# A fourth store tile, and weight splits of two pairs, in a kernel of 496 pairwise products

## The chip, the cores and the metric

The kernel runs on one core of a Trainium2 chip. The metric is the device time of one execution in microseconds (us). Five runs of the kernel before took 775.05 to 776.29 us, median 775.73.

## The reference

Each of 1024 samples has 32 fields of 128 numbers. For every pair of fields i < j (496 pairs) with a weight matrix of its own, field i goes through the matrix and the result is multiplied by field j, element by element:

```python
pairs = list(itertools.combinations(range(32), 2))
v_i = inputs[:, I_IDX, :]                    # (1024, 496, 128)
v_j = inputs[:, J_IDX, :]
transformed = jnp.einsum('bpd,ped->bpe', v_i, W)   # W: (496, 128, 128)
return transformed * v_j
```

The output, 1024 x 496 x 128 numbers of float32, is 260 MB. Everything else is small beside it: 32.5 MB of weights and 16.8 MB of input.

## The kernel before

**Layout.** The host hands over x transposed, one slab of 128 x 1024 for each field (d by sample), and the weights in the order in which the kernel uses them, four pairs to a transfer. All slabs of x stay in SBUF. The pairs are taken by rows: i runs down from 30 to 0, and for each i all j above it, so that the rows grow from 1 pair to 31. A pair is worked on in two halves of 512 samples; such a half is a unit u, and pair q has the units 2q and 2q + 1.

**Products.** The first 15 pairs (i from 30 to 26) are multiplied in float32 as they are (L148). All others use a faster number format in three matmuls: x and the weights are each split in a high part, a low part and a combination of both (h, l, d). In `first(u)` TensorE multiplies h by h and l by l into one PSUM bank (two matmuls, L151), and ScalarE scales the bank (L152). In `second(u)`, three units later (LAG = 3), TensorE adds the product of the d parts (L160), and VectorE multiplies the bank by x of field j into the store tile (L166). There are eight PSUM banks.

**Splits.** `split_w(c)` makes h, l and d for a chunk c of WC = 4 pairs: one ScalarE instruction for h (L92), then three of GpSimd (L93 for l, L94 and L95 for d), each 128 x 512. The three results are tiles of the pool `ws`, three tiles each. `split_x(f, a)` does the same for half a slab of x (L106 to L109), in the pool `xs`, two tiles each. All splits stand in the list `todo` with the pair from which they may be put out and the pair that needs them (L117 to L123). The list is sorted by need. After every odd unit at most one split is put out: the first in the list that may be. A split of chunk c may be put out from pair (c - 2) * WC + 1, that is 4c - 7, seven pairs ahead of pair 4c.

**Stores and loads.** A store tile `ot` holds two pairs (OG = 2), 128 x 2 x 1024, 1 MB. The pool `o` has three of them (L64). When VectorE has written the fourth product into it, SyncE issues its store (L170); the last two pairs are stored by halves (L168). SyncE also issues the loads of weights (L83, 256 KB for four pairs, in the pool `wr` of five tiles, four transfers ahead) and of x (L74, some rows ahead), all in one queue in order of program.

**Order.** From `tc.manual_schedule()` on, each engine executes its instructions in the order in which the loop over u writes them. What an engine waits for follows from the tiles: a store tile is written again when its last store has landed, a PSUM bank when VectorE has read it, a raw weight tile is loaded again when all its splits have read it.

**SBUF**, in KB of a partition: x 128, `xs` 24, `wr` 10, `ws` 18, `o` 24, together 204.

Of the kernel before, what the change touches and what calls it, by code (L numbers as in the profile page):

```python
# [1 line left out]

# [4 lines left out]

F32 = mybir.dt.float32
F32R = mybir.dt.float32r
ALU = mybir.AluOpType  # L10

P = 128
NF = 32
NQ = NF * (NF - 1) // 2
BT = 1024
HB = 512
WC = 4
WL = 4
OG = 2
EPS = 2.0**-12  # L20
NATIVE = 5
LAG = 3
WLEAD = 4
XLEAD = 3


def _pairs():

    return [(i, j) for i in range(NF - 2, -1, -1) for j in range(i + 1, NF)]


@with_exitstack
def kernel(
    ctx: ExitStack,
    tc: tile.TileContext,
    xt: bass.AP,
    wt: bass.AP,
    out: bass.AP,
):

    nc = tc.nc
    pairs = _pairs()
    nchunk = NQ // WC

    xpool = ctx.enter_context(tc.tile_pool(name="x", bufs=1))  # L60
    spool = ctx.enter_context(tc.tile_pool(name="xs", bufs=2))
    rpool = ctx.enter_context(tc.tile_pool(name="wr", bufs=5))
    wpool = ctx.enter_context(tc.tile_pool(name="ws", bufs=3))
    opool = ctx.enter_context(tc.tile_pool(name="o", bufs=3))  # L64
    ppool = ctx.enter_context(tc.tile_pool(name="ps", bufs=8, space=bass.MemoryType.PSUM))

    x_sb = {}

    def load_x(f, n=1, pieces=1, eng=None):

        t = xpool.tile([P, n, BT], F32, tag=f"x{f}", name=f"x_{f}")
        s = BT // pieces
        for k in range(pieces):
            (eng or nc.sync).dma_start(out=t[:, :, k * s : (k + 1) * s], in_=xt[:, f : f + n, k * s : (k + 1) * s])  # L74
        for k in range(n):
            x_sb[f + k] = t[:, k, :]

    w_raw = {}

    def load_w(c, splits=(0, WL)):  # L80
        w_raw[c] = rpool.tile([P, WL, P], F32, tag="w", name=f"w_{c}")
        for a, b in zip(splits, splits[1:]):
            nc.sync.dma_start(out=w_raw[c][:, a:b, :], in_=wt[c, :, a:b, :])  # L83

    w_s = {}

    def split_w(c):

        k = c * WC % WL
        raw = w_raw[c * WC // WL][:, k : k + WC, :].rearrange("p q e -> p (q e)")  # L90
        h, l, d = [wpool.tile([P, WC * P], F32R, tag=t, name=f"{t}_{c}") for t in ("wh", "wl", "wd")]
        nc.scalar.mul(h, raw, 1.0 - 2.0**-13)  # L92
        nc.gpsimd.tensor_tensor(l, raw, h.bitcast(F32), ALU.subtract)  # L93
        nc.gpsimd.tensor_scalar(d, h.bitcast(F32), EPS, 1.0, ALU.mult, ALU.mult)  # L94
        nc.gpsimd.tensor_tensor(d, l.bitcast(F32), d.bitcast(F32), ALU.subtract)  # L95
        w_s[c] = (h, l, d)

    x_s = {}

    def split_x(f, a):  # L100

        if a == 0:
            x_s[f] = [spool.tile([P, BT], F32R, tag=t, name=f"{t}_{f}") for t in ("xh", "xl", "xd")]
        s = slice(a, a + HB)
        h, l, d = [t[:, s] for t in x_s[f]]
        nc.scalar.mul(h, x_sb[f][:, s], 1.0 - 2.0**-13)  # L106
        nc.gpsimd.tensor_tensor(l, x_sb[f][:, s], h.bitcast(F32), ALU.subtract)  # L107
        nc.gpsimd.tensor_scalar(l, l.bitcast(F32), 1.0 / EPS, 1.0, ALU.mult, ALU.mult)  # L108
        nc.gpsimd.tensor_tensor(d, h.bitcast(F32), l.bitcast(F32), ALU.subtract)  # L109

    nq0 = NATIVE * (NATIVE + 1) // 2
    c0 = nq0 // WC
    first_q = {i: q for q, (i, j) in reversed(list(enumerate(pairs)))}

    todo = []  # L117
    for c in range(c0, nchunk):
        todo.append(((c - 2) * WC + 1, max(c * WC, nq0), lambda c=c: split_w(c)))
    for i in range(NF - 2 - NATIVE, -1, -1):  # L120
        for a in range(0, BT, HB):
            todo.append((first_q[i + 1] + 1 if i < NF - 3 - NATIVE else 2, first_q[i], lambda i=i, a=a: split_x(i, a)))
    todo.sort(key=lambda t: t[1])  # L123

    load_w(0, (0, 1, WL))
    load_x(NF - 2, pieces=2, eng=nc.scalar)
    load_x(NF - 1, pieces=2, eng=nc.scalar)
    load_x(NF - 3)
    load_x(NF - 4)
    load_w(1)  # L130
    for f in range(NF - 5, NF - 4 - XLEAD, -1):
        load_x(f)
    load_w(2)
    load_w(3)


    ctx.enter_context(tc.manual_schedule())
    po, ots = {}, {}


    def first(u):
        q, h = divmod(u, 2)
        i, c = pairs[q][0], q // WC
        r = slice(q % WC * P, (q % WC + 1) * P)
        s = slice(h * HB, (h + 1) * HB)
        po[u] = ppool.tile([P, HB], F32, tag="po", name=f"po_{u}")
        if q < nq0:
            nc.tensor.matmul(po[u], w_raw[q // WL][:, q % WL, :], x_sb[i][:, s], start=True, stop=True)  # L148
        else:
            for t in (0, 1):  # L150
                nc.tensor.matmul(po[u], w_s[c][t][:, r], x_s[i][t][:, s], start=t == 0, stop=t == 1)  # L151
            nc.scalar.mul(po[u], po[u], 1.0 + EPS)  # L152

    def second(u):
        q, h = divmod(u, 2)
        i, j = pairs[q]
        r = slice(q % WC * P, (q % WC + 1) * P)
        s = slice(h * HB, (h + 1) * HB)
        if q >= nq0:
            nc.tensor.matmul(  # L160
                po[u], w_s[q // WC][2][:, r], x_s[i][2][:, s], start=False, stop=True, skip_group_check=True
            )
        g, k = divmod(q, OG)
        if k == 0 and h == 0:
            ots[g] = opool.tile([P, OG, BT], F32, tag="ot", name=f"ot_{g}")
        nc.vector.tensor_tensor(ots[g][:, k, s], po.pop(u), x_sb[j][:, s], ALU.mult)  # L166
        if q >= NQ - 2:
            nc.sync.dma_start(out=out[g, :, k, s], in_=ots[g][:, k, s])  # L168
        elif k == OG - 1 and h == 1:
            nc.sync.dma_start(out=out[g], in_=ots[g])  # L170

    for u in range(2 * NQ + LAG):
        q = u // 2
        if u % (2 * WL) == 0 and (q // WL + WLEAD) * WL < NQ:
            load_w(q // WL + WLEAD)
        if u < 2 * NQ:
            i, j = pairs[q]
            if u % 2 == 0 and j == i + 1 and 0 <= i - 2 - XLEAD:
                load_x(i - 2 - XLEAD)
            first(u)  # L180
        if u >= LAG:
            second(u - LAG)
        if u % 2 == 1:
            ready = [t for t in todo if t[0] <= q]
            if ready:
                ready[0][2]()
                todo.remove(ready[0])
    assert not todo


# [25 lines left out]
```

## Time and profile before

| | before |
|---|---|
| median of five runs | 775.73 us |
| the profiled execution | 775.73 us |
| its span, first to last instruction | 773.9 us |
| moved by DMA | 310.04 MB, 260.05 written and 49.28 read in HBM |
| stores L170: count, size, issue to landing | 247, 1024 KB, 6.2 us |
| weight loads L83 | 123, 256 KB, 6.0 us |
| VectorE's product L166 | 992 of 684 ns |
| ScalarE's scaling L152 | 962 of 580 ns |
| ScalarE's split L92, 128 x 512 | 121 of 626 ns |
| GpSimd's split L93, L94, L95, 128 x 512 | 121 each, of 1289, 618 and 1295 ns |
| GpSimd's split of x, L107, L108, L109 | 52 each, of 1288, 619 and 1288 ns |

The profile is of one execution. A busy time counts the time in which an engine had an instruction running; instructions that follow each other closely overlap a little, so that four L166 of 684 ns take 2.48 us. PE is TensorE's matmuls, PEld its weight loads, DVE VectorE, ACT ScalarE, POOL GpSimd, SPq the queue of SyncE. In tables of waits each line says who waited (its line and tile), for whose result, and then the us in total, the number of waits and the longest. The DMA share of a stretch is the mean busy share of 16 DMA engines; it can be a little over 1, since packets overlap.

### The profile page before, as it was taken

The numbers are of one execution on the slowest core, as the hardware profiler recorded it, in microseconds if no ns is written. First come the engines' busy times: TensorE is split into PE (matmuls) and PEld (weight loads), VectorE is DVE, ScalarE is ACT, GpSimd is POOL, SyncE is SP. The second block draws the span as 40 slices with busy tenths as digits, with TensorE's granted clock in tenths as the row PEclk, the third lists the DMA queues.
The fourth block names the chain that finished last, engine by engine and source line by source line (L and its number), as shares of the span: only waits on it lengthen the run. The fifth ranks groups of instructions, "written<-read, shape, count | busy, mean of one in ns | idle before, by whom it ended". The sixth has DMA issues, their size and how long they took to land.

```text
span 773.9 us, 10983 instructions
## 1 busy us (share of the span) xinstructions
PE 719.1 (93%) x2946; PEld 549.8 (71%) x2946; DVE 617.6 (80%) x992; ACT 619.6 (80%) x1136; POOL 549.9 (71%) x523
## 2 busy tenths in 40 slices
PE   8979899998989999999998999898999999999996
PEld 3557676766767777677676877686877777777774
DVE  4668777777887787787787888787888888888886
ACT  2268788888968888888887888797998888888884
POOL 1978899887768767867767585767686859585550
PEclk9999999999999999999999999999999999999998
DMA  9999999999999999999999999999999999999998
GB/s 357 375 408 378 408 413 408 399 395 396 398 397 404 389 410 406 412 397 412 398 413 370 416 401 409 386 404 389 417 408 416 415 404 416 412 401 417 402 402 364
DMA packets 59101, 310.04 MB, mean 401 GB/s; under 512 B 6560, under 2 KB 6816, under 8 KB 27424
## 3 DMA queue, kind: packets, MB, share of 16 engines
q1 hardware_dynamic: 58464, 308.31, 99.2%
q10 hardware_dynamic: 576, 1.05, 0.4%
q8 instruction: 23, 0.38, 0.2%
q14 instruction: 38, 0.31, 0.1%
HBM read 49.28 MB, written 260.05 MB: 400 GB/s over the span
## 4 chain that ended last, share of the span: by engine, by line
DMA 47%; PE 30%; DVE 20%; issue 1%; DVEq 0%
DMA out_dram<-ot 47%; DVE ot L166 20%; PE po L151 20%; PE po L160 9%; PE po L148 1%; DMA x<-in_xt_dram 0%; DVEq L166 0%; DVEq L209 0%
## 5 line engine op out<-in xcount | busy, mean ns | idle before, releaser
L166 DVE TENSOR_TENSOR ot<-po,x 128x512 f32<-128x512 f32 x992 | 617.6, 684 | 150.4 <-DMA out_dram<-ot 105.4
L152 ACT ACTIVATE po<-po 128x512 f32<-128x512 f32 x962 | 540.6, 580 | 129.7 <-PE po L151 82.6
L151 PE MATMUL po<-xh,wh 128*128 128x512 f32 x962 | 390.3, 406 | 42.3 <-DVE ot L166 40.6
L151 PE MATMUL po<-xl,wl 128*128 128x512 f32 x962 | 379.1, 394 | 1.0 <-POOL wl L93 1.0
L160 PE MATMUL po<-xd,wd 128*128 128x512 f32 x962 | 378.6, 394 | 0.0
L151 PEld LDWEIGHTS po<-xh,wh 128*128 128x128 f32 x962 | 182.2, 189 | 122.6 <-DVE ot L166 84.0
L93 POOL TENSOR_TENSOR wl<-w,wh 128x512 fp32r<-128x512 f32 x121 | 156.0, 1289 | 154.0 <-ACT wh L92 154.0
L160 PEld LDWEIGHTS po<-xd,wd 128*128 128x128 f32 x962 | 182.4, 190 | 40.4 <-ACT po L152 0.4
L151 PEld LDWEIGHTS po<-xl,wl 128*128 128x128 f32 x962 | 182.7, 190 | 34.2 <-POOL wl L93 1.5
L95 POOL TENSOR_TENSOR wd<-wl,wd 128x512 fp32r<-128x512 f32 x121 | 156.7, 1295 | 10.1
L107 POOL TENSOR_TENSOR xl<-x,xh 128x512 fp32r<-128x512 f32 x52 | 67.0, 1288 | 22.8 <-ACT xh L106 22.8
L94 POOL TENSOR_SCALAR wd<-wh 128x512 fp32r<-128x512 f32 x121 | 74.8, 618 | 10.2
L92 ACT ACTIVATE wh<-w 128x512 fp32r<-128x512 f32 x121 | 75.8, 626 | 2.1 <-DMA w<-in_wt_dram 2.1
L109 POOL TENSOR_TENSOR xd<-xh,xl 128x512 fp32r<-128x512 f32 x52 | 67.0, 1288 | 4.3
L106 ACT ACTIVATE xh<-x 128x512 fp32r<-128x512 f32 x52 | 32.7, 630 | 11.7 <-DMA x<-in_xt_dram 11.6
L108 POOL TENSOR_SCALAR xl<-xl 128x512 fp32r<-128x512 f32 x52 | 32.2, 619 | 4.6
L148 PE MATMUL po<-x,w 128*128 128x512 f32 x60 | 28.0, 629 | 3.8 <-DMA x<-in_xt_dram 3.8
L148 PEld LDWEIGHTS po<-x,w 128*128 128x128 f32 x60 | 12.0, 202 | 18.9 <-issue 13.2
L106 ACT ACT_TABLE_LOAD x1 | 1.3, 1283 | 2.6 <-issue 2.6
L203 POOL MEMSET const-float32-0.0<- 128x1 f32 x1 | 0.1, 98 | 0.2 <-issue 0.2
L203 POOL MEMSET const-bfloat16-1.0<- 128x1 bf16 x1 | 0.1, 101 | 0.0
L203 POOL MEMSET const-uint8-127<- 128x1 uint8 x1 | 0.1, 101 | 0.0
(1 smaller groups left out, 0.1 us busy)
## 6 DMA issues: line engine op xcount, KB each, us to landing
out_dram<-ot SPq DMA_DIRECT2D x247, 1024.0 KB, 6.2
w<-in_wt_dram SPq DMA_DIRECT2D x123, 256.0 KB, 6.0
x<-in_xt_dram SPq DMA_DIRECT2D x30, 512.0 KB, 7.5
x<-in_xt_dram ACTq DMA_DIRECT2D x4, 256.0 KB, 4.7
out_dram<-ot SPq DMA_DIRECT2D x4, 256.0 KB, 4.6
w<-in_wt_dram SPq DMA_DIRECT2D x1, 192.0 KB, 3.5
w<-in_wt_dram SPq DMA_DIRECT2D x1, 64.0 KB, 2.7
```

The lines of the kernel that those rows point to most:

```text
L92: nc.scalar.mul(h, raw, 1.0 - 2.0**-13)
L93: nc.gpsimd.tensor_tensor(l, raw, h.bitcast(F32), ALU.subtract)
L94: nc.gpsimd.tensor_scalar(d, h.bitcast(F32), EPS, 1.0, ALU.mult, ALU.mult)
L95: nc.gpsimd.tensor_tensor(d, l.bitcast(F32), d.bitcast(F32), ALU.subtract)
L106: nc.scalar.mul(h, x_sb[f][:, s], 1.0 - 2.0**-13)
L107: nc.gpsimd.tensor_tensor(l, x_sb[f][:, s], h.bitcast(F32), ALU.subtract)
L109: nc.gpsimd.tensor_tensor(d, h.bitcast(F32), l.bitcast(F32), ALU.subtract)
L148: nc.tensor.matmul(po[u], w_raw[q // WL][:, q % WL, :], x_sb[i][:, s], start=True, stop=True)
L151: nc.tensor.matmul(po[u], w_s[c][t][:, r], x_s[i][t][:, s], start=t == 0, stop=t == 1)
L152: nc.scalar.mul(po[u], po[u], 1.0 + EPS)
L160: nc.tensor.matmul(po[u], w_s[q // WC][2][:, r], x_s[i][2][:, s], start=False, stop=True, skip_group_check=True)
L166: nc.vector.tensor_tensor(ots[g][:, k, s], po.pop(u), x_sb[j][:, s], ALU.mult)
```

## The change

- A chunk of split weights has two pairs instead of four (WC = 2). There are 241 splits in place of 121, each with the same four instructions, now 128 x 256.
- The pool `ws` has four tiles of each part in place of three: eight pairs of split weights in place of twelve, 12 KB a partition in place of 18.
- A split may be put out from pair (c - 3) * WC + 1, now 2c - 5, five pairs ahead of pair 2c.
- The pool `o` has four store tiles in place of three, 32 KB in place of 24. Together 206 KB in place of 204.

Loads (WL = 4 pairs to a transfer), stores, matmuls, L152 and L166 are the same in number and size.

```diff
-WC = 4
+WC = 2
...
-    wpool = ctx.enter_context(tc.tile_pool(name="ws", bufs=3))
-    opool = ctx.enter_context(tc.tile_pool(name="o", bufs=3))
+    wpool = ctx.enter_context(tc.tile_pool(name="ws", bufs=4))
+    opool = ctx.enter_context(tc.tile_pool(name="o", bufs=4))
...
-        todo.append(((c - 2) * WC + 1, max(c * WC, nq0), lambda c=c: split_w(c)))
+        todo.append(((c - 3) * WC + 1, max(c * WC, nq0), lambda c=c: split_w(c)))
```

## The prediction

> **What bounds the kernel now.** I read the page first, then the waits, then stretches of 2 us. Busy shares and the chain of waits:
>
> ```profile
> PE 719.1 (93%) x2946; PEld 549.8 (71%) x2946; DVE 617.6 (80%) x992; ACT 619.6 (80%) x1136; POOL 549.9 (71%) x523
> ...
> DMA packets 59101, 310.04 MB, mean 401 GB/s; under 512 B 6560, under 2 KB 6816, under 8 KB 27424
> ...
> DMA out_dram<-ot 47%; DVE ot L166 20%; PE po L151 20%; PE po L160 9%; PE po L148 1%; DMA x<-in_xt_dram 0%; DVEq L166 0%; DVEq L209 0%
> ```
>
> No compute engine sets the end alone: 47% of the chain is stores, and the DMA row of the page is 9 in nearly every slice. The table of waits says who feels it (us in total, times, longest):
>
> ```profile
> DVE ot L166 <- DMA out_dram<-ot: 105.4, 113, 4.2
> PEld po L151 <- DVE ot L166: 84.0, 117, 3.8
> ...
> PE po L151 <- DVE ot L166: 40.6, 35, 3.4
> ...
> PEld po L151 <- POOL wl L93: 1.5, 1, 1.5
> ...
> PE po L151 <- POOL wl L93: 1.0, 1, 1.0
> ```
>
> VectorE has no free store tile, TensorE no free PSUM bank behind it; GpSimd's splits cost TensorE only 2.5 us. But a wait for a transfer is worth something only if the DMA engines stand idle because of it later. The stretches of 2 us around the longest such wait show that (columns: busy us and instructions of PE, PEld, DVE, ACT, POOL, granted clock, DMA share, GB/s):
>
> ```profile
> 412.00:414.00 2.00, 2.00 (x11) 1.65 (x10) 2.00 (x4) 2.00 (x5) 1.90 (x3) 1.00 1.00 416
> 414.00:416.00 2.00, 1.92 (x9) 1.26 (x7) 0.33 (x1) 1.90 (x5) 1.93 (x2) 1.00 1.03 434
> 416.00:418.00 2.00, 0.00 (x0) 0.00 (x0) 0.00 (x0) 0.32 (x1) 1.83 (x3) 1.00 1.00 410
> 418.00:420.00 2.00, 0.72 (x3) 0.61 (x4) 1.46 (x3) 0.00 (x0) 1.92 (x3) 1.00 1.03 434
> 420.00:422.00 2.00, 2.00 (x8) 1.61 (x7) 2.00 (x4) 1.30 (x3) 1.85 (x2) 0.70 0.38 156
> 422.00:424.00 2.00, 2.00 (x6) 1.56 (x5) 1.47 (x3) 1.30 (x3) 0.00 (x0) 0.50 1.05 365
> ```
>
> While TensorE and VectorE stand still (414 to 419) the DMA runs at 410 to 434 GB/s: the wait itself costs nothing. The price comes after: the queue has emptied, TensorE starts again at half clock, and the DMA share falls to 0.38. So the bound is the DMA, and what can be had is the time in which it is not fed. I went through all stretches of 2 us from 28 to 768 us: 16 have a share under 0.90, and lack 7.2 us in all; 4 of the 7 under 0.80 have a lowered TensorE clock like this one. Another 54 have a share of 0.95 or more, yet under 390 GB/s; against the median stretch (414) they lose 16 us. Their cause no view names.
>
> **The fourth store tile (line 64).** A tile cycles through filling and storing. The median store lands 6.2 us after its issue, and four VectorE products take 2.48 us back to back, so three tiles give 8.7 us for six pairs, 1.45 us a pair against 1.56 (773.9 / 496) measured: the ring is only just long enough and any late store shows. A fourth adds 1 MB of queue, 2.5 us at 417 GB/s. It removes no byte: the best stretches of 20 us move 417 GB/s, and 310.04 MB at that rate is 743 us, a floor. I count the 7.2 us of missing share as what it can win, less the 2.3 us of it that lie before 160 us, where GpSimd gets in the way (below): **-5 us**. Of the 16 us of slow stretches the bounds are 0 (they come whatever the queue holds) and -16 (they come from a short queue). In the trace's packet records an 8 KB packet usually takes 309 ns, and in those stretches up to 606, twice that, as if a packet had no successor to overlap with; they sit mostly just ahead of a load that was issued behind a short queue. That speaks for the queue, only as a correlation: I take a third, **-5 us**.
>
> The Trainium skill speaks against any gain here: "DMA: Bandwidth & Descriptors", Specifications, gives a limit of about 358 GB/s of HBM for one core, by which nothing could be won, and a fabric ceiling of 435 GB/s, by which the floor would be 713 us. The trace's mean of 401 GB/s is above the first, so I don't count by it.
>
> **The finer splits (lines 17, 63, 119).** 121 splits of four pairs become 241 of two; each is one ScalarE and three GpSimd instructions, so 120 and 360 more instructions. No DMA is added. GpSimd's timeline at one piece of x and the split after it:
>
> ```profile
> 94.74 1.29 POOL L107 TENSOR_TENSOR xl<-x,xh 128x512 fp32r<-128x512 f32 x1
> 96.12 0.62 POOL L108 TENSOR_SCALAR xl<-xl 128x512 fp32r<-128x512 f32 x1
> 96.82 1.30 POOL L109 TENSOR_TENSOR xd<-xh,xl 128x512 fp32r<-128x512 f32 x1
> 98.07 1.30 POOL L93 TENSOR_TENSOR wl<-w,wh 128x512 fp32r<-128x512 f32 x1
> ```
>
> From 94.74 to 98.07 is 3.33 us for a split (2 x 1.29 + 0.62 + 0.13 of gaps). At 256 columns there is no row. Bounds: half of everything, 1.67 us, and no saving, 3.33 us. The nearest row for a fixed part is a MEMSET of one column, 98 to 101 ns: (1.29 - 0.10) / 2 + 0.10 = 0.70 and (0.62 - 0.10) / 2 + 0.10 = 0.36 us, so 2 x 0.70 + 0.36 + 0.13 = **1.88 us, 0.94 a pair** (0.83 before). GpSimd grows by 241 x 1.88 - 121 x 3.33 = 50 us, to some 600 of 774; the mean doesn't matter, the short rows at the start do. A row of n pairs costs it 6.67 us for two pieces of x and 0.94 n. The first L151 matmul of the rows of 6, 7, 8 ... pairs starts at 31.2, 42.0, 56.3, 69.1, 84.8, 99.5, 116.7, 136.1 and 156.3 us. Against these lengths (10.8, 14.3, 12.8, 15.7, 14.7 ...) GpSimd needs 12.3, 13.3, 14.2, 15.1, 16.1: its debt grows to 2.7 us at the row of 10, and is paid back by the row of 13. Before, 11.7, 12.5, 13.3, 14.2, 15.0 made a debt of 0.9 at most.
>
> The Trainium skill has a dearer price: "GPSIMD Engine Reference", 3.1, gives 4497 ns for a TENSOR_TENSOR of 2048 columns; with the 1289 ns of this trace at 512 that is an estimate of 754 ns at 256, a split of about 2.04 us, and a debt near 6 us instead of 2.7. No row here shows which holds.
>
> The lead shrinks with it. A split was put out 7 pairs ahead of its need (after unit 8c - 13, needed at 8c), now 5 (after 4c - 9, needed at 4c): 9 half-pairs, 7.0 us at 773.9 / 992 = 0.78. The worst order in a long row is piece, split, piece, split, one a pair: the second split starts at 3.33 + 1.88 + 3.33 = 8.5 us after the first piece, has its wl at 9.3, and TensorE wants it at 4.7 + 7.0 = 11.7. Some 2 us are left; before, the worst order was piece, piece, split, its wl at 6.67 + 1.29 = 8.0, wanted at 3.1 + 13 x 0.78 = 13.2, 5 us left. So now the debt of the short rows does become a wait of TensorE, in part hidden by the 2.5 us more queue: I count **+3 us** (0 to +8; the last is the debt of a split of 2.1 us, with nothing hidden).
>
> ScalarE: L92 at 256 columns is bounded by 313 and 626 ns (row: 626 at 512), 0 to 75 us more in all. Two pairs then cost it four L152 at 0.53 (back to back) and one L92, 2.7 us at most of 3.1; it waits 82.6 us for TensorE now, which hides it. Queued behind a waiting L92 or L93 are the L152 of the next pair and the next split; ring slots are free by program order (wd of chunk c - 4 is read one unit before split c is put out). SyncE: a raw weight tile is released by its second half-split, after unit 8c - 13 instead of 8c - 21; SyncE reaches the load at 8c - 2, 11 units or 8.6 us later, against some 5 us of lag plus 1.9. The next store is due 4 units after, so a load that waits a little holds nothing. Both at nothing; without that cover a store is late by what the load waits.
>
> **Sum.** 773.9 - 5 - 5 + 3 = 766.9 of span; the execution's own time was 775.73 with a span of 773.9, 1.8 beside it, and equals the median of the five runs (775.73). **768.7, say 768 us.**
>
> **Rivals.** *A, forecast:* the queue no longer runs dry, 768; from 752 (all 7 and 16 us won, GpSimd hidden) to 774. For it: share 0.38 after a stall. *B, no change:* the slow stretches stay, and what the tile wins after 160 us is spent on GpSimd's debt before it: 773.9 - 5 + 5 + 1.8 = 776. For it: the share is 0.9 or more in 354 of 370 stretches; against: 7 of the gaps have a plain cause. *C, slower:* GpSimd sets the pace of the rows of 6 to 15 pairs. They last 201.8 - 31.2 = 170.6 us now; GpSimd needs 10 x 6.67 + 105 x (split / 2). At 2.17 us a split that is 10 us more than now, as much as A wins: from there on it decides. At 2.3 us it is 187.5, +17 - 10, 783. For it: POOL is busy 19.0 of the 20 us from 100 to 120 us; against: 1.88. *D:* the change can't fail to be done: the tile is allocated, 206 KB a partition instead of 204.
>
> **Numbers.** What the measurement tells from no change is 0.2%, 1.6 us. A 0.62, B 0.14, C 0.24, with faster, same and slower alike. The range takes A whole and B, and of C what the bounds +8 and a gain of 2 make: 773.9 - 2 + 8 + 1.8 = 782, cut to 780 since both ends would have to meet: 752 to 780.
>
> **What would show it.** Right: DVE waits on out_dram fall from 105 to under 70 us, stores land later than 6.2 us (8 or more) since more are queued, fewer half-clock stretches, L93 near 0.70 us. Wrong in A: under 743 us, or stretches under 0.80 as many as before. C: TensorE's waits on POOL wl rise from 2.5 to over 15 us before 200 us, L93 above 0.83 us.

## The result, and the profile after

The changed kernel takes 771.7 us (median; 769.5 to 776.8), the kernel before, in turn with it on the same chips, 774.8. The ratio is 0.9965, 95% interval 0.9955 to 0.9974: faster by 0.35%, or 2.7 us (the medians differ by 3.1). The forecast was 768 us from 775.7. The sign is the forecast's, the size is little more than a third of it.

The page of the changed kernel: busy times, DMA totals, and the chain of work that ended last, by engine.

```profile
PE 716.3 (93%) x2946; PEld 551.6 (72%) x2946; DVE 627.0 (81%) x992; ACT 633.7 (82%) x1256; POOL 611.5 (79%) x883
...
DMA packets 59108, 310.11 MB, mean 403 GB/s; under 512 B 6560, under 2 KB 6816, under 8 KB 27424
...
DMA 51%; PE 26%; DVE 16%; POOL 5%; issue 1%; DVEq 0%; SPq 0%; POOLq 0%
...
out_dram<-ot SPq DMA_DIRECT2D x247, 1024.0 KB, 8.9
```

GpSimd has grown from 549.9 to 611.5 us and now stands in the chain with 5%. The mean rate is 403 GB/s in place of 401. A store lands 8.9 us after its issue (6.2 before): the queue is as much longer as one more tile makes it. Its table of waits (us in total, times, longest):

```profile
DVE ot L166 <- DMA out_dram<-ot: 76.7, 85, 3.9
...
PEld po L151 <- DVE ot L166: 52.8, 84, 2.7
...
PEld po L151 <- POOL wl L93: 21.0, 15, 2.7
...
PE po L151 <- POOL wl L93: 14.9, 14, 2.3
```

VectorE waits less for store tiles (105.4 before). TensorE now waits 35.9 us for GpSimd's wl, against 2.5. What a split costs GpSimd stands in its timeline (start, length in us, then the instruction):

```profile
642.16 0.74 POOL L93 TENSOR_TENSOR wl<-w,wh 128x256 fp32r<-128x256 f32 x1
642.98 0.40 POOL L94 TENSOR_SCALAR wd<-wh 128x256 fp32r<-128x256 f32 x1
643.47 0.74 POOL L95 TENSOR_TENSOR wd<-wl,wd 128x256 fp32r<-128x256 f32 x1
644.17 0.74 POOL L93 TENSOR_TENSOR wl<-w,wh 128x256 fp32r<-128x256 f32 x1
```

From 642.16 to 644.17 a split takes 2.01 us; 1.88 was forecast. The start of the first L151 matmul of a row shows where the time goes (from both timelines, us):

| row of | 10 | 13 | 17 | 23 | 26 | 31 |
|---|---|---|---|---|---|---|
| after minus before | -3.7 | +2.8 | -4.0 | -4.4 | -8.7 | -7.6 |

Between the rows of 10 and 13 the changed kernel loses 6.5 us, by the row of 17 it has them back, and then it gains slowly. TensorE's last four L160, first of the kernel before and then of the changed one:

```profile
764.93 1.33 PE L160 MATMUL po<-xd,wd 128*128 128x512 f32 x4
```

```profile
757.46 1.33 PE L160 MATMUL po<-xd,wd 128*128 128x512 f32 x4
```

Here the gain is still 7.5 us, near the -7 that the prediction had summed up (-5 -5 +3). But the span ends only 4.5 us earlier (773.9 to 769.4). The last windows of 1 us say why (columns: busy us of PE, PEld, DVE, ACT, POOL, granted clock, DMA share, GB/s); the kernel before:

```profile
771.00:772.00 1.00, 0.00 (x0) 0.00 (x0) 0.00 (x0) 0.00 (x0) 0.00 (x0) 0.50 0.85 318
772.00:773.00 1.00, 0.00 (x0) 0.00 (x0) 0.00 (x0) 0.00 (x0) 0.00 (x0) 0.50 0.07 25
```

and the changed one:

```profile
764.00:765.00 1.00, 0.00 (x0) 0.00 (x0) 0.00 (x0) 0.00 (x0) 0.00 (x0) 0.50 0.85 313
765.00:766.00 1.00, 0.00 (x0) 0.00 (x0) 0.00 (x0) 0.00 (x0) 0.00 (x0) 0.50 0.15 55
766.00:767.00 1.00, 0.00 (x0) 0.00 (x0) 0.00 (x0) 0.00 (x0) 0.00 (x0) 0.50 0.06 25
767.00:768.00 1.00, 0.00 (x0) 0.00 (x0) 0.00 (x0) 0.00 (x0) 0.00 (x0) 0.50 0.06 25
```

A share of 0.06 is 1/16: one DMA engine of sixteen is still at work, alone, for more than 2 us. The trace also notes when each sixteenth of a transfer has landed. Over the transfers that landed from 300 to 600 us, the last sixteenth came 1.5 us after their median in the kernel before, and 4.2 us after it in the changed one. I call this the **lag**. A store tile is free when the last sixteenth is out. So the fourth tile lets the other engines run one store further ahead of the slowest: a tile is some 2.5 us of queue, and the lag grew by 2.7. At the end they wait for it. (From 600 us on the last sixteenth but one came about 1 us after the median, so at the end it is one engine; from 200 to 550 us a second one was late as well, by 2.7 to 3.8 us.) Of the 7.5 us in the body of the profile, 3.0 were only this running ahead.

The stretches of 2 us, counted as in the prediction (from 28 us on, the last 8 us left out): those with a DMA share under 0.90 lacked 7.2 us and now lack 5.8; those with a share of 0.95 or more and under 390 GB/s lost 16.3 us and now lose 11.9. All stretches together, by their bytes, fell short of 414 GB/s by 20.3 us and now do by 13.2, which fits the 7.5 us. The gaps at 218, 420, 494, 530 and 750 us are gone, others have come, among them this one, in which GpSimd's debt has let the queue run dry and TensorE starts again at half clock:

```profile
134.00:136.00 2.00, 1.28 (x3) 1.09 (x4) 0.02 (x1) 0.45 (x1) 1.83 (x4) 0.66 0.99 416
136.00:138.00 2.00, 2.00 (x6) 1.52 (x6) 1.36 (x2) 0.72 (x2) 1.83 (x4) 0.50 1.03 435
138.00:140.00 2.00, 2.00 (x10) 1.66 (x9) 1.60 (x3) 1.72 (x4) 1.83 (x4) 0.98 0.53 203
```

### The profile page after: what moved, and what is told of

The parts are those of the page before. It is cut to its first block, busy times and chain, and to the rows that moved or that the text cites. A ratio compares the mean times of both kernels' runs of the same rounds, so it can differ in the third digit from the quotient of the medians.

```text
span 769.4 us, 11797 instructions
## 1 busy us (share of the span) xinstructions
PE 716.3 (93%) x2946; PEld 551.6 (72%) x2946; DVE 627.0 (81%) x992; ACT 633.7 (82%) x1256; POOL 611.5 (79%) x883
## 4 chain that ended last, share of the span: by engine, by line
DMA 51%; PE 26%; DVE 16%; POOL 5%; issue 1%; DVEq 0%; SPq 0%; POOLq 0%
DMA out_dram<-ot 50%; DVE ot L166 16%; PE po L151 15%; PE po L160 7%; PE po L148 4%; POOL xd L109 2%; POOL wl L93 1%; POOL xl L107 1%; POOL wd L95 1%; DMA x<-in_xt_dram 0%; POOL xl L108 0%; POOL wd L94 0%; DVEq L166 0%; SPq L74 0%; DVEq L209 0%
## 5 line engine op out<-in xcount | busy, mean ns | idle before, releaser
L166 DVE TENSOR_TENSOR ot<-po,x 128x512 f32<-128x512 f32 x992 | 627.0, 685 | 134.1 <-DMA out_dram<-ot 76.7
L152 ACT ACTIVATE po<-po 128x512 f32<-128x512 f32 x962 | 549.1, 583 | 110.0 <-PE po L151 61.0
L151 PE MATMUL po<-xh,wh 128*128 128x512 f32 x962 | 386.8, 402 | 22.6 <-DVE ot L166 21.4
L151 PE MATMUL po<-xl,wl 128*128 128x512 f32 x962 | 380.7, 396 | 15.9 <-POOL wl L93 14.9
L160 PE MATMUL po<-xd,wd 128*128 128x512 f32 x962 | 378.0, 393 | 0.0
L151 PEld LDWEIGHTS po<-xh,wh 128*128 128x128 f32 x962 | 182.2, 189 | 91.6 <-DVE ot L166 52.8
L93 POOL TENSOR_TENSOR wl<-w,wh 128x256 fp32r<-128x256 f32 x241 | 177.9, 738 | 73.5 <-ACT wh L92 73.5
L151 PEld LDWEIGHTS po<-xl,wl 128*128 128x128 f32 x962 | 182.8, 190 | 56.8 <-POOL wl L93 21.0
L160 PEld LDWEIGHTS po<-xd,wd 128*128 128x128 f32 x962 | 182.5, 190 | 39.1 <-ACT po L152 0.4
L95 POOL TENSOR_TENSOR wd<-wl,wd 128x256 fp32r<-128x256 f32 x241 | 177.8, 738 | 20.1
L94 POOL TENSOR_SCALAR wd<-wh 128x256 fp32r<-128x256 f32 x241 | 97.4, 404 | 20.3
L92 ACT ACTIVATE wh<-w 128x256 fp32r<-128x256 f32 x241 | 99.1, 412 | 0.0
L109 POOL TENSOR_TENSOR xd<-xh,xl 128x512 fp32r<-128x512 f32 x52 | 67.0, 1289 | 4.3
L106 ACT ACTIVATE xh<-x 128x512 fp32r<-128x512 f32 x52 | 32.5, 629 | 11.9 <-DMA x<-in_xt_dram 11.8
```

Source lines behind the costliest of these rows:

```text
L160: nc.tensor.matmul(po[u], w_s[q // WC][2][:, r], x_s[i][2][:, s], start=False, stop=True, skip_group_check=True)
```

## The experiments

Two figures from the packet records go with each: the lag as above, and the number of **long packets**, those of the 31,616 packets of 8 KB (all stores are made of them but the last) that took over 400 ns instead of some 309.

Each ratio is to runs of the kernel before that were measured together with that kernel.

| kernel | median, us | ratio to before, 95% interval | span of the profile | lag, us | long packets |
|---|---|---|---|---|---|
| before | 774.8 | 1 | 773.9 | 1.5 | 1355 |
| after | 771.7 | 0.9965 (0.9955 to 0.9974) | 769.4 | 4.2 | 922 |
| splits only, 3 tiles | 778.5 | 1.0055 (1.0034 to 1.0075) | 774.1 | 1.3 | 1643 |
| light splits, 4 tiles | 772.4 | 0.9973 (0.9951 to 0.9995) | 770.1 | 4.4 | 1006 |
| light splits, 3 tiles | 773.5 | 0.9986 (0.9972 to 1.0000) | 771.4 | 1.5 | 1330 |
| no d product | 765.8 | 0.9893 (0.9857 to 0.9929) | 764.5 | 4.3 | 897 |
| no d product, more fetches | 766.4 | 0.9890 (0.9869 to 0.9911) | 760.6 | 4.1 | 588 |
| weights as 120 + 8 partitions | 790.6 | 1.0198 (1.0163 to 1.0232) | 789.1 | not worked out | 1855 |
| weights as 64 + 64 partitions | 782.3 | 1.0085 (1.0067 to 1.0103) | 780.6 | 3.2 | 1388 |
| weights in 4 KB packets | 774.4 | 1.0005 (0.9992 to 1.0018) | 773.5 | 4.5 | 1105 |
| VectorE and transfers, 4 tiles | 759.2 | 0.9827 (0.9770 to 0.9885) | 757.4 | 4.2 | 574 |
| VectorE and transfers, 3 tiles | 765.5 | 0.9874 (0.9837 to 0.9911) | 762.5 | 1.3 | 877 |
| transfers alone | 769.7 | 0.9932 (0.9906 to 0.9957) | 763.6 | 10.2 | 1022 |
| stores alone | 635.8 | 0.8203 (0.8191 to 0.8216) | 634.2 | 0.5 | 6 |
| transfers alone, loads in a second queue | 752.3 | 0.9707 (0.9692 to 0.9722) | 750.4 | 0.3 | 309 |
| native rows of 6 and 7 | 768.1 | 0.9913 (0.9880 to 0.9946) | 764.2 | 4.2 | 814 |
| the same, weights by ScalarE's queue | 767.8 | 0.9900 (0.9886 to 0.9914) | 765.7 | 3.8 | 503 |

### The two parts of the change

The first theory (S) was that one DMA engine sets the pace once the queue is long; the rival (G) that GpSimd's dearer splits eat the gain. The first edit makes the splits-only kernel, the second the light splits, which leave out L94 (d = l - h), both the light splits with three tiles.

```diff
-    opool = ctx.enter_context(tc.tile_pool(name="o", bufs=4))
+    opool = ctx.enter_context(tc.tile_pool(name="o", bufs=3))
...
-        nc.gpsimd.tensor_scalar(d, h.bitcast(F32), EPS, 1.0, ALU.mult, ALU.mult)
-        nc.gpsimd.tensor_tensor(d, l.bitcast(F32), d.bitcast(F32), ALU.subtract)
+        nc.gpsimd.tensor_tensor(d, l.bitcast(F32), h.bitcast(F32), ALU.subtract)
```

> The changed kernel with three store tiles, so the finer splits alone. Two theories of where the gain of the fourth tile went. Theory S (one slow DMA engine): one of the 16 DMA engines has more to do than the others and is busy nearly all the time; a store has landed only when its share has; in the changed kernel its backlog is still being worked off from 765 to 768 us at a DMA share of 0.06, one sixteenth. Theory G (GpSimd): the dearer splits (2.02 us for two pairs) took back what the tile won, 6.5 us between the rows of 10 and 13 pairs. Here G says: the splits alone cost 6 us or more, ratio to before 1.008 or above. S says: every wait on GpSimd that the shallow queue can't hide reaches the slow engine, 2 to 6 us, 1.003 to 1.008. Both agree on the sign; the run prices the splits.

> The changed kernel without L94: d is l minus h instead of l minus EPS times h, one GpSimd instruction fewer for a split (2.02 to about 1.53 us, 0.77 a pair, below the 0.83 of before). G: the 6.5 us come back, ratio to before 0.985 to 0.989. S: only the time comes back in which the slow engine stood idle before 150 us (about 4.5 us of it in the changed kernel), ratio 0.991 to 0.995, and the last stage keeps its pace of 1.44 us a pair.

> The kernel after without L94 (d is l - h; a part of the computation is left out) and with three store tiles: it completes the four of three or four tiles by normal or light splits. S (what the finer splits cost with three tiles, +0.55%, is GpSimd's dearer price): back to the kernel before, ratio 0.998 to 1.002, and GpSimd's rows hold no wait. Rival (the cost comes from the shorter ring and the later release of raw weights, whatever GpSimd takes): 1.004 to 1.007, as the splits alone.

The finer splits alone cost 0.55%, 4.3 us, as S had it (0.3 to 0.8%). With L94 left out and three tiles that cost is gone (0.9986). TensorE's waits for wl with splits only (three tiles):

```profile
PEld po L151 <- POOL wl L93: 15.5, 12, 2.7
...
PE po L151 <- POOL wl L93: 11.1, 10, 2.2
```

and with light splits and three tiles:

```profile
PEld po L150 <- POOL wl L93: 0.9, 2, 0.7
...
PE po L150 <- POOL wl L93: 0.2, 1, 0.2
```

So the cost of the finer splits is GpSimd's time. The 120 more instructions of ScalarE, the shorter ring and the later release of raw weights, which are all still there, cost nothing that shows. (A light split of two pairs takes GpSimd 1.51 us, a little less for each pair than the 3.33 us for four of the kernel before.)

The four kernels also price the fourth tile. With the splits as they are it is worth 0.9965 / 1.0055 = 0.991 (0.989 to 0.993 with both intervals), some 7 us. With light splits it is worth 0.9973 / 0.9986 = 0.999 (0.996 to 1.001): nothing that could be told from no change. (Four tiles with splits of four pairs, 212 KB a partition, were not tried.) By these ratios most of what the tile wins in the changed kernel is what the waits for GpSimd cost that the other half of the change brought in. (The waits themselves stay, 26.6 us with three tiles and 35.9 with four; that a longer queue covers them is argued from the ratios.) The traces add that the tail takes its share in both pairs: when 308 MB have moved, the kernel with four tiles is 7.1 us ahead of the one with three (light splits: 3.6), but its span is only 4.7 us shorter (1.3). G as it was put falls too: with GpSimd's extra work gone again, four tiles are not faster than the kernel after. Both S (0.991 to 0.995 here) and G had hoped for more.

### Is it TensorE's instruction fetch?

One queue of the profile carries TensorE's instructions: 24 blocks of 16 KB, 0.98 us each. If they all fell on the engine that lags, that would be its burden. In the first kernel L94, L95, L109 and the matmul L160 are left out; in the second the edit below is added.

```diff
-            for t in (0, 1):
-                nc.tensor.matmul(po[u], w_s[c][t][:, r], x_s[i][t][:, s], start=t == 0, stop=t == 1)
+            for a in (0, HB // 2):
+                e = slice(h * HB + a, h * HB + a + HB // 2)
+                nc.tensor.matmul(
+                    po[u][:, a : a + HB // 2], w_s[c][0][:, r], x_s[i][0][:, e], start=True, stop=False,
+                    skip_group_check=True,
+                )
+            nc.tensor.matmul(
+                po[u], w_s[c][1][:, r], x_s[i][1][:, s], start=False, stop=True, skip_group_check=True
+            )
```

> The changed kernel without the d product: L94, L95, L109 and the matmul L160 are left out, so TensorE has a third less to do and GpSimd more than half less. All stores and loads are as they are. If the DMA engines together are the bound (310 MB at the 417 GB/s of the best stretches, 743 us) or TensorE or GpSimd is, the span falls to 745 to 752, ratio 0.963 to 0.973. S: TensorE fetches 3968 instructions instead of 5892, some 7.5 of 23 fetches of 16 KB fewer, each 0.98 us on one DMA engine: 7 us less there, and the idle time before 150 us gone: span 757 to 763, ratio 0.979 to 0.986.

> The kernel without the d product (765.8 us, 15 blocks of TensorE instructions of 16 KB fetched), with the first matmul of L151 cut in two of 256 columns: 962 matmuls and weight loads more, the same multiplications, some 7.5 more blocks to fetch, 22 or 23 as in the kernel after. S with its engine named (the lagging DMA engine is the one that also fetches TensorE's instructions): 7.5 x 0.97 = 7.3 us back on that engine, 771 to 775 us, ratio 0.995 to 1.001, and one engine alone works in the last 3 us. Rival (the fetches fall on an engine with room, or the gain came from less TensorE work): 764 to 768, ratio 0.987 to 0.992, TensorE being far from its limit (635 of 764 us busy before the cut).

The first, at 0.9893, came nearer to S than to the theory that compute or all engines together set the time, but lies above both bands (0.979 to 0.986 and 0.963 to 0.973): with a third of the matmuls gone and GpSimd at 276 us, only 6 us go. The second was the test of the engine named, and it failed: 23 blocks instead of 15, and no time (0.9890 beside 0.9893). The fetches are not what makes an engine lag. (What the second kernel computes is no longer the same; number and size of its instructions are as said.)

### Fewer or more packets for the engines

Two kernels cut each load of weights in two transfers, of 120 and 8 partitions or of 64 and 64 (the first edit); a third loads eight pairs at a time (the others).

```diff
-            nc.sync.dma_start(out=w_raw[c][:, a:b, :], in_=wt[c, :, a:b, :])
+            for p, n in ((0, 120), (120, 8)):
+                nc.sync.dma_start(out=w_raw[c][p : p + n, a:b, :], in_=wt[c, p : p + n, a:b, :])
...
-WL = 4
-WLEAD = 4
+WL = 8
+WLEAD = 2
-    rpool = ctx.enter_context(tc.tile_pool(name="wr", bufs=5))
+    rpool = ctx.enter_context(tc.tile_pool(name="wr", bufs=3))
+    dpool = ctx.enter_context(tc.tile_pool(name="wd", bufs=3))
```

> The changed kernel with each weight load issued as two transfers, of partitions 0 to 119 and 120 to 127, the same bytes. A transfer of 120 rows can be shared out on 15 engines, one of 8 rows on 8, so the last engine gets no weights (32.5 MB / 16 at 26.5 GB/s is 77 us of work less for it) and eight others get a ninth more (9.6 us). S: if the slow engine is the last one, the time falls to 755 to 763, ratio 0.975 to 0.985; if it is one of those eight, it rises by about 9 us, 1.005 to 1.012; else it stays within 2 us of the changed kernel. G, or all engines together as the bound: no gain, and 125 more transfers can only cost, 0.996 to 1.003.

> The kernel after, with each load of weights issued as two transfers of 64 partitions: the same 125 transfers more as with 120 + 8 partitions, but all 16 DMA engines get the same number of packets as before. S (one DMA engine lags, and in the 120 + 8 run it was among the eight that got a ninth packet): the lagging engine gets only one 4-byte packet more for each load, 125 x 0.009 = 1 us; 771 to 777 us, ratio to the kernel before 0.995 to 1.003. Rival (more transfers cost by themselves, which engine gets the packets is nothing): as slow as with 120 + 8, 787 to 793 us, ratio 1.015 to 1.023.

> The kernel after with weights loaded eight pairs at a time (62 transfers of 512 KB with packets of 4 KB in place of 124 of 256 KB with packets of 2 KB), three raw tiles of eight pairs for five of four, and three wd tiles for four to make room. Stores and products as in the kernel after. S (every DMA engine, the lagging one too, is busy to the end, so its packets' time is the time): 1016 packets of 84 ns become 508 of 159, 4.6 us less an engine, and 0.5 us less of 4-byte packets; 765 to 769 us, ratio 0.987 to 0.993. Rival (the pace is not that of the DMA engines' packets): 770 to 774, ratio 0.994 to 0.999; a price beside both is GpSimd's wait for a wd tile, up to 2 us in the short rows.

With as many transfers in both, the uneven cut is 790.6 - 782.3 = 8.3 us slower than the even one: how a load is cut matters, which fits packets that stay with the engine they were given to (a ninth packet on eight engines had been put at 9 us). It is not shown: the records don't name a packet's engine. The uneven cut lies above every band named for it, and the even cut missed its band too (782 for 771 to 777): the split first loads feed TensorE late, and the first 10 MB have moved 7 us after those of the kernel before. As a proof that one and the same engine lags, the pair is not enough.

The 4 KB packets won nothing. The edit had brought a wait of its own, with three wd tiles instead of four (its table of waits):

```profile
POOL wd L99 <- PE po L164: 74.6, 110, 1.8
...
PEld po L155 <- POOL wl L98: 28.7, 21, 2.7
...
PE po L155 <- POOL wl L98: 20.7, 18, 2.3
```

TensorE's waits for wl rose to 49.4 us, so this run tells nothing about packets.

### The floor, measured by itself

Theory F: the transfers' own floor lies far above 743 us. Rival U: fed without a gap, they run at the rate of the best stretches. In VectorE and transfers all of first(u), L160 and the splits are left out and the first edit is made; in the transfers alone the second edit stands in its place, four tiles that are filled once.

```diff
-        nc.vector.tensor_tensor(ots[g][:, k, s], po.pop(u), x_sb[j][:, s], ALU.mult)
+        nc.vector.tensor_tensor(ots[g][:, k, s], x_sb[i][:, s], x_sb[j][:, s], ALU.mult)
...
+            if g < 4:
+                ots[g] = opool.tile([P, OG, BT], F32, tag=f"ot{g}", name=f"ot_{g}")
+                nc.vector.memset(ots[g], 1.0)
+            else:
+                ots[g] = ots[g % 4]
```

> The kernel after with the matmuls, the scaling and all splits left out: VectorE multiplies x of field i by x of field j straight from SBUF into the store tiles; every load and store is there, in the same order in SyncE's queue, with four store tiles. F (the transfers' own floor lies far above the 743 us that were reckoned from the best stretches of 20 us, so a longer queue soon has nothing more to win): 756 to 768 us, ratio to the kernel before 0.975 to 0.992. Rival U (fed without a gap the transfers run at the 417 GB/s of the best stretches, and the rest of the time after is TensorE and GpSimd): 743 to 751 us, ratio 0.959 to 0.970.

> The same with three store tiles. F: without TensorE's and GpSimd's waits there is nothing for the fourth tile to bridge: within 3 us of four tiles. Rival, as the prediction had it (a short queue in itself costs DMA time, whatever keeps it short: a third or more of the 16 us of slow stretches): 5 to 12 us slower than four tiles.

> The same without VectorE's products: four tiles are filled once and stored again and again, so no store waits for any engine. All transfers of the kernel after, nothing else. F: 752 to 765 us, ratio 0.970 to 0.988, at most 6 us less than with VectorE and four tiles. U: 738 to 748, ratio 0.952 to 0.966.

With VectorE's products and four tiles the transfers take 759.2 us (0.9827; three runs at 759, one at 770): in F's band, far from U's. With no matmul, no split and no wait for a tile they take 769.7 us (0.9932), 0.3% less than the kernel after. U is out, and for this kernel F had still thought too little (0.970 to 0.988, and not more than with VectorE's products). Stretches of the transfers alone (columns: busy us of DVE and POOL, granted clock, DMA share, GB/s):

```profile
100.00:150.00 50.00, 0.00 (x0) 0.00 (x0) 1.00 1.02 424
150.00:200.00 50.00, 0.00 (x0) 0.00 (x0) 1.00 1.01 417
...
700.00:750.00 50.00, 0.00 (x0) 0.00 (x0) 1.00 1.01 410
```

and its end:

```profile
752.00:753.00 1.00, 0.00 (x0) 0.00 (x0) 1.00 0.50 199
753.00:754.00 1.00, 0.00 (x0) 0.00 (x0) 1.00 0.23 96
...
757.00:758.00 1.00, 0.00 (x0) 0.00 (x0) 1.00 0.06 25
...
761.00:762.00 1.00, 0.00 (x0) 0.00 (x0) 1.00 0.06 25
```

A store lands 15.3 us after its issue, against 8.9 in the kernel after:

```profile
out_dram<-ot SPq DMA_DIRECT2D x247, 1024.0 KB, 15.3
```

The queue is never short here, and yet the rate falls from 424 to 410, the lag grows to 10.2 us, there are about as many long packets as in the kernel after, and in the last 6 us one engine works nearly alone. So neither compute nor a short queue is needed for them. Nor is 769.7 a floor: the same transfers, filled by VectorE, were 10 us faster. In the first 150 us, while the lag is small, there are 3 long packets in all, though loads and stores alternate from the start.

The Trainium skill bears on the rate: "HBM Reference", Specifications, says that a core that streams alone reaches some 425 GB/s. The 424 of this run's 100 to 150 us agree with it, its later 410 and the 403 of the kernel after do not reach it.

The pair of VectorE and transfers prices the tile a third time: 0.9827 / 0.9874 = 0.995 (0.988 to 1.002), 6.3 us between the medians, 5.1 between the profiled spans. That is the lower edge of the prediction's reading and more than the 3 us that F allowed; the interval takes in the 0.991 and the 0.999 of above, so it decides nothing by itself.

### Loads among stores

What makes the engines part? L1: one engine is slower at any traffic. L2: loads and stores meeting. L3: their order in one queue. Stores alone leaves the loads of the loop out, as below; the other kernel issues all loads with nc.scalar.dma_start.

```diff
-        if u % (2 * WL) == 0 and (q // WL + WLEAD) * WL < NQ:
-            load_w(q // WL + WLEAD)
-            if u % 2 == 0 and j == i + 1 and 0 <= i - 2 - XLEAD:
-                load_x(i - 2 - XLEAD)
```

> The transfers alone without the loads of weights and of x in the loop (only those ahead of it are left): 260 MB of stores out of four tiles, nothing else. L1 (one DMA engine is slower at any traffic, by the 2.6% that it lacked in the transfers alone: 10 us of lag built up in some 300 us and then held, one engine alone for the last 6 us): its lag builds up again, and the last 3 us or more of the profile have a share of 0.06 to 0.08. L2 (the lag comes from loads and stores meeting on one engine): the engines stay together, no such tail, and 260 MB take 32 packets of 309 ns for each store pair, 247.5 x 2.48 = 614 us, so 622 to 634 us in all, ratio 0.803 to 0.820. L1: 634 to 648, ratio 0.820 to 0.837.

> The transfers alone, with all loads issued in ScalarE's queue and the stores in SyncE's. Nothing is computed. L1: the same engine lags, 762 to 774 us as with one queue, ratio 0.985 to 0.998. L3 (it is the one queue, with its order of loads between stores, in which the lag builds up): the engines stay together or the loads fill the others' idle time, 745 to 758, ratio 0.962 to 0.978.

Stores alone, two stretches and the end:

```profile
100.00:150.00 50.00, 0.00 (x0) 0.00 (x0) 1.00 1.01 419
300.00:350.00 50.00, 0.00 (x0) 0.00 (x0) 1.00 1.01 419
```

```profile
630.00:631.00 1.00, 0.00 (x0) 0.00 (x0) 1.00 1.09 367
631.00:632.00 1.00, 0.00 (x0) 0.00 (x0) 1.00 1.04 338
632.00:633.00 1.00, 0.00 (x0) 0.00 (x0) 1.00 0.35 127
```

The rate holds at 419, the engines end together, 6 long packets in 31,616, lag 0.5: no engine is slower at stores by itself, and L1 is out. (An engine that is slower at loads alone would look the same; no run has loads alone.) (By its time, 635.8 us, the run stands at the edge between L2's 622 to 634 and L1's 634 to 648; the marks decide: no lag that builds up, no tail.) The loads in a queue of their own gave the time that L3 had named (752.3), but not for its reason. Nothing reads the weights in this kernel, so the second queue ran ahead, and all loads were through by 250 us:

```profile
200.00:250.00 50.00, 0.00 (x0) 0.00 (x0) 1.00 1.02 389
250.00:300.00 50.00, 0.00 (x0) 0.00 (x0) 1.00 1.01 426
300.00:350.00 50.00, 0.00 (x0) 0.00 (x0) 1.00 1.01 420
```

As long as loads and stores meet, 389 to 412 GB/s (from 50 us on) and all but 5 of the 309 long packets; from then on stores alone, at 420. That fits L2 once more. The lag of 0.3 in the table is that of the stores alone; from 50 to 200 us, while the two met, it was 1.7 to 2.0. L3 is left to the full kernel, below.

Now the prediction's 743 us can be understood. Stores alone move 264.27 MB in 635.8 us. The transfers alone move 45.1 MB more; at 419 GB/s that is 107.7 us, together 743.5. So 743 is what all bytes would take if those of loads cost no more than those of stores. They took 769.7 (765.4 to 773.8): here the loads among the stores cost 22 to 30 us more than their bytes. With VectorE filling the tiles (759.2) it is some 16, with all loads in the first 250 us (752.3) some 9.

### A version that beats both

The gap from 32 to 36 us, where the first row with splits begins, is deeper after the change than before (its share lacks 2.5 us, 1.6 before), and GpSimd's debt comes next. Both hang on the short rows. The edit on NATIVE and its due time makes the first kernel, the last one (L83) is added in the second.

```diff
-NATIVE = 5
+NATIVE = 7
-            todo.append((first_q[i + 1] + 1 if i < NF - 3 - NATIVE else 2, first_q[i], lambda i=i, a=a: split_x(i, a)))
+            todo.append((first_q[i + 1] + 1 if i < NF - 3 - NATIVE else first_q[i + 4], first_q[i], lambda i=i, a=a: split_x(i, a)))
...
-            nc.sync.dma_start(out=w_raw[c][:, a:b, :], in_=wt[c, :, a:b, :])
+            (nc.scalar if c >= WLEAD else nc.sync).dma_start(out=w_raw[c][:, a:b, :], in_=wt[c, :, a:b, :])
```

> The kernel after with the rows of 6 and 7 pairs multiplied in float32 as they are, as the first 15 pairs (NATIVE 7 for 5): no splits for them, so GpSimd starts on the row of 8 with a lead instead of a debt. TensorE: 30 of these products took 28.2 us, 26 more are 24.4 us, against 25.1 us that the two rows take in the kernel before (31.2 to 56.3). G2 (GpSimd's debt in the rows of 6 to 13 is what the change lost: 6.5 us between the rows of 10 and 13 in its profile): 3 to 6 us of it come back, 766 to 769 us, ratio 0.988 to 0.9935. F (the transfers make up for a late start whatever happens, since they lag behind anyway): 770 to 773, ratio 0.994 to 0.998.

> The kernel with native rows of 6 and 7 pairs, with the loads of weights in the loop issued in ScalarE's queue in place of SyncE's. L1: no change beside it, 766 to 770 us, ratio 0.988 to 0.9935. L3: 3 us or more below it, 758 to 765, ratio 0.978 to 0.987. A price beside both: each of 120 issues holds ScalarE's queue, and stores and loads no longer land in one order.

768.1 us, 0.9913: faster than both kernels, by some 0.5% than the one after (0.9913 / 0.9965 = 0.995, 0.991 to 0.998 with both intervals). The stretch that had been a gap, in the kernel before:

```profile
32.00:34.00 2.00, 0.96 (x6) 0.44 (x4) 0.93 (x2) 1.07 (x2) 1.92 (x3) 1.00 0.67 283
34.00:36.00 2.00, 2.00 (x9) 1.58 (x9) 1.82 (x4) 1.41 (x3) 1.92 (x3) 1.00 0.55 161
```

in the kernel after:

```profile
32.00:34.00 2.00, 2.00 (x10) 1.64 (x9) 0.74 (x2) 1.32 (x4) 1.83 (x4) 1.00 0.68 287
34.00:36.00 2.00, 2.00 (x11) 1.64 (x10) 1.70 (x3) 2.00 (x6) 1.83 (x4) 1.00 0.05 16
```

and with seven native rows:

```profile
32.00:34.00 2.00, 2.00 (x6) 0.95 (x5) 1.50 (x4) 0.00 (x0) 0.34 (x1) 1.00 0.98 406
34.00:36.00 2.00, 2.00 (x6) 0.89 (x5) 1.66 (x3) 0.72 (x2) 0.57 (x1) 1.00 1.04 434
```

Its 25th megabyte is out 3 us sooner than after the change. So G2's band is met, but half of the reason is another: 3 us come from this gap, and TensorE still waits 28.1 us for wl.

The weights in ScalarE's queue change nothing (0.9900, intervals overlap; the loads of x stayed with the stores), and L3, which had named 3 us or more, is out for the weights: where the loads can't run ahead, a queue of their own doesn't keep them from meeting the stores. The Trainium skill says so, "DMA: Bandwidth & Descriptors", section "Issuing engines are not separate DMA queues": transfers that different engines start run on the same 16 DMA engines and mix there. This run agrees with it, at 0.9900 beside 0.9913.

## Why the prediction was right or wrong

**The bound**, the DMA, was right: with all matmuls, scaling and splits left out the transfers still take 759.2 us, with VectorE's products left out too 769.7; the kernel after takes 771.7.

**The step that failed** is the term of the fourth tile: "It removes no byte: the best stretches of 20 us move 417 GB/s, and 310.04 MB at that rate is 743 us, a floor. I count the 7.2 us of missing share as what it can win". The tile was put at -10 us. With the finer splits it measured about -7 (0.991), with the light ones about -1, which can't be told from nothing (0.999). The best stretches were no measure for the whole: that rate is the rate of stores alone (419), and with the loads among them no run came near 743 (759.2 and 769.7 in the kernel's order, 752.3 with the loads ahead). And the share is a mean over sixteen engines, while a tile comes free with the slowest. Taken apart, kernel after against kernel before:
- *Missing share, -5:* 7.2 us became 5.8, -1.4. Before 160 us, where GpSimd's debt lies, 2.3 became 4.4: the gap at 34 us is deeper, and the one at 138 us is new. After 160 us, which is what the term counted, 4.9 became 1.4: the five later gaps are gone and one at 294 us has come. But with finer splits and three tiles only 1.0 is left there too, so this is not shown to be the tile's work.
- *Slow stretches, -5:* 16.3 us became 11.9, -4.3. The size was right. The reason was half right: a longer ring has fewer long packets (1355 to 922, and 877 to 574 without compute), but a short queue is not needed for them, since a queue that is never short has 1022.
- *Not forecast, +3.0:* the tail. The other engines run ahead by the tile that was added, and the end waits for the slowest.

Three pairs of kernels differ in the fourth tile alone. Their profiles, one of each kernel, show what it took off each term (us, three tiles to four, counted as in the prediction):

| pair | missing share | slow stretches | span |
|---|---|---|---|
| finer splits | 5.7 to 5.8 | 15.3 to 11.9 | 774.1 to 769.4 |
| light splits | 6.0 to 5.1 | 15.6 to 11.1 | 771.4 to 770.1 |
| VectorE and transfers | 5.4 to 0.8 | 13.9 to 11.0 | 762.5 to 757.4 |

So with TensorE at work the tile takes no more than 1 us off the missing share, where 5 had been counted; only where no engine but VectorE computes does that term come out. The slow stretches shrink by 3 to 4.5 us in all three.

**The finer splits, +3 (0 to +8):** about right, +4.3 by themselves. A split costs 2.01 us, not 1.88: L93 takes 738 ns where 700 was worked out from the one-column MEMSET row, L94 404 where it was 360. So the debt was larger, and 6.5 us were lost between the rows of 10 and 13, 5.0 of them in the row of 10, where the prediction had the debt at its largest.

The page that had the dearer price was nearer. The Trainium skill, "GPSIMD Engine Reference", 3.1, led to an estimate of 754 ns and a debt near 6 us; 738 and 6.5 were measured.

**ScalarE and SyncE at nothing:** right. L92 takes 412 ns, between the bounds of 313 and 626. The light splits with three tiles keep all of that and cost nothing.

**The sum** was -7; measured are -4.5 in the profiled executions and -2.7 by the ratio, which is the tile's -7 and the splits' +4.3. That the body of the profile comes out at -7.5 is luck in part, since the terms in it came out otherwise. The prediction let the longer queue hide some of the splits' cost, but counted the tile's win in full beside it: by the ratios most of the tile's 7 us are the splits' 4.3, bridged. Where nothing had to be bridged its worth could not be told from nothing (0.999 with light splits, 0.995 with an interval up to 1.002 without compute).

**The rivals.** 771.7 lies about midway between A's 768 and B's 776; C's 783 did not come. B's mechanism, that what the tile wins is spent on GpSimd's debt, did a good part of the work. C's first mark was met, waits for wl before 200 us of 25.9 us where 15 were named. Its second was not (L93 0.74 where 0.83 us was named), and a split took 2.01 us, below the 2.17 from which C was to decide.

**The marks.** Stores land at 8.9 us: met. Waits for store tiles 76.7 where 70 was named: nearly. Fewer half-clock stretches: hardly, 10 with a clock under 0.95 in place of 11. Stretches with a share under 0.80: 4 for 7, but two more stand in the tail (one before).

**Still open:** why loads among stores put the engines out of step. The first 150 us of the transfers alone show that mixing alone isn't enough: there the two alternate at 424 GB/s with 3 long packets. Whether it is always the same engine that comes last, and whether one is slower at loads, the records don't say.

## What to carry to other kernels

A floor for transfers is measured, not read off the best stretches: the same transfers with the computation left out are one short kernel. Here two such kernels gave 759 and 770 us where the best stretches had given 743, so how the queue is fed counts too, and one run of this kind is not yet a floor. A DMA share is a mean over sixteen engines; look at when the last sixteenth of a transfer lands and at the last us of the span, where a share of 1/16 means one engine alone. And when an edit pays for one resource with another engine's time, the two terms are not added: here most of what the longer queue won were the waits that came with it.

## What the hardware showed that was not expected

- A queue that is never short is not the fastest. With VectorE filling four tiles (stores land after 8.9 us) the transfers took 759.2 us, ratio 0.9827 (0.9770 to 0.9885); with no store waiting for an engine (they land after 15.3 us) 769.7, ratio 0.9932 (0.9906 to 0.9957), and a lag of 10.2 us in place of 4.2. Why is not shown.
- Loads of 45 MB among stores of 260 MB cost more than their bytes, 22 to 30 us with a queue that is never short, some 16 with VectorE filling the tiles; stores alone keep 419 GB/s and a lag of 0.5 us.
- One matmul of 512 columns in every product cut in two, with 8 blocks of instructions more to fetch (23 for 15), cost nothing: 0.9890 beside 0.9893, TensorE 634.0 us busy beside 635.4.
